# A group of four sorted lanes for one of five: expert weights through SyncE at a row held in a register

## The chip, the cores and the metric

The kernel runs on one core of one Trainium2 chip. The metric is the device time of the run in microseconds (us), and the figure quoted is the median of three runs. Engines are named as the profile names them: PE is TensorE's matrix multiply and PEld its weight load, DVE is VectorE, ACT is ScalarE, POOL is GpSimd, and SP is SyncE, which does nothing here but issue transfers.

## The reference

A decoder of two layers works on x of 16 sequences x 128 tokens x 256 features in float32, with residual additions. Everything but the last step is the same before and after the change; the last step is the one that the change is about.

```python
x = x + attention(layernorm(x), qk, ov)             # layer 0: one head, causal
x = x + cross_attention(layernorm(x), ctx, mask)    # 16 heads of 16
x = x + block_ffn(layernorm(x))                     # router over 16 blocks of 64, the best 4 kept
x = x + (self_attention(layernorm(x)) + b_o + layernorm(x))   # layer 1: 16 heads
x = x + windowed_attention(layernorm(x), cell)      # windows of 64, rotary, causal and same cell
x = x + moe(layernorm(x))

def moe(x):                                         # x: (2048, 256)
    scores = sigmoid(x @ gate.T)                    # 8 experts
    w, idx = top_k(scores, 2);  w = 2.5 * w / w.sum(-1)
    g, u = einsum('th,eih->tei', x, w_gate), einsum('th,eih->tei', x, w_up)    # i: 128
    y = einsum('tei,ehi->teh', silu(g) * u, w_down)
    routed = einsum('te,teh->th', one_hot_weights(w, idx), y)
    return routed + swiglu(x, ws_gate, ws_up, ws_down)          # shared expert of width 256
```

Each token needs two of the eight experts.

## The kernel before

**Lanes and threads.** The 16 sequences are eight lanes of two (`NL`, `G`), so that a lane is 256 tokens. Each lane goes through layer 0 and layer 1. In Python every lane's layer is a generator, called a thread here, which yields the name of the engine that it wants next and the buffers that it needs for that step. The class `Turns` holds these threads while the kernel is built. It keeps a model of when each engine comes free (`free_at`), when each thread can go on (`th.at`), and when each buffer of a kind comes free. `Turns.run` takes, over and over, the thread with the lowest key, lets it issue its step, and charges the modelled cost: `SWITCH` for a change of the matmul's shape, `HOP` for a passage from one engine to another, `RELEASE` for a buffer's return. So the order of every engine's queue is written out when the kernel is built, and on the chip each engine works through its queue in that order, waiting where an operand is late.

Before the change, `key` lets a thread that holds or asks for an attention score buffer (`first`) go ahead by `LEAD` = 100 ns. `LIMITS` gives how many buffers there are of each kind: five `xn` (normalised tokens), three `qs` (masked queries), six `p`. The buffers `p` of 128 x 1024 float32 serve three users: the attention's exponentials, a tile of the experts (as `we`), and a lane's gathered results (as `yg`).

**Which lanes run at once.** `more` begins lane-layers in the order `TURN`: layer 0 of lanes 0 to 5, then by turns layer 1 of a lane and layer 0 of a later one. Up to `IN_FLIGHT` = 6 lane-layers run at once. A masked query or a rotated key needs a swap of neighbouring rows, which is a transfer that SP issues (`q.load`, line 189, buffer `swap`). So SP's queue holds the swaps, the loads of mask rows, and the stores of results.

**The experts.** There are two ways. A lane that is in no group goes dense: `expert_ffn` multiplies all of its 256 tokens by all eight experts and both halves of the shared one (`gu`), weights each expert's hidden values by `wb`, and adds the ten products of `y`. A lane in `GROUPS` goes sorted. `routing` ranks its experts, multiplies 0/1 selections into counts (`n`) and scatters each token's row twice into `to_experts` in memory, with four indirect transfers that POOL issues (`q.indexed`, line 168). The shared expert is a thread of its own (`shared`). When the last lane of the group has been routed, `sorted_experts` starts. Its `plan` is a row of small DVE steps that finds, for each tile of 128 rows, the expert and the first row; it leaves `tile_rows` and `tile_weights`, one index for each partition. Then all tiles start at once as threads of `expert_tile`. Five lanes make 27 tiles: 5 x 256 x 2 rows are 20 tiles, and 7 more are needed because every expert's rows begin a new tile.

A tile takes one `p` buffer. POOL first gathers the expert's weights into three quarters of it, by `tile_weights`, and then the tokens into the last quarter, by `tile_rows`. PE transposes the tokens (`xgt`), multiplies gate and up (`gu2`), transposes the hidden values (`hT2`) and multiplies down (`y2`). ACT copies the result over the tokens and stores it to `by_experts` on its own queue. When all tiles are stored, `combining` gathers four times per lane from `by_experts` (`yg`, by POOL), and DVE adds each, weighted, to `x`; SP stores the lane's output (line 1194, and line 1336 for a dense lane).

**Lines.** Most operations go through helpers of `Turns`, so the profile shows the helper's line: L135 a matmul, L140 a transpose, L144 DVE, L149 ACT, L155 POOL, L168 an indirect transfer, L189 a load or store.

Of the kernel before, what the change touches and what calls it, by code (L numbers as in the profile page):

```python
# [17 lines left out]
B, S, D = 16, 128, 256  # L18
P = 128
# [11 lines left out]
BPC = P // 64  # L31
NE, TOPE = 8, 2

GROUPS = ((0, 1, 2, 3, 4),)


OUT = -(2.0**100)
# [37 lines left out]
PE, DVE, ACT, POOL, SP = "PE", "DVE", "ACT", "POOL", "SP"  # L75
# [6 lines left out]
class Turns:  # L82
# [3 lines left out]

    LEAD = 100.0
    HOP = 70.0  # L90
    HOP_FROM_PE = 200.0
    SWITCH = 91.0
    PART = 20.0
    RELEASE = 30.0

    def __init__(self, nc, limits):
        self.nc = nc
# [22 lines left out]
    def shaped(self, shape):  # L120

        if shape != self.shape:
            self.shape = shape
            self.charge(PE, self.SWITCH)

# [31 lines left out]
    def moved(self, n_bytes):  # L157

        self.moves = max(self.moves, self.now.at) + n_bytes / 300.0
        self.now.at = self.moves + 2000.0  # L160

    def indexed(self, out, out_index, src, src_index):

        at = lambda i: None if i is None else bass.IndirectOffsetOnAxis(ap=i, axis=0)
        self.charge(POOL, 1050.0)
        self.moved(4 * int(np.prod((src if src_index is None else out).shape)))
        self.now.at += 2000.0
        self.nc.gpsimd.indirect_dma_start(out, at(out_index), src, at(src_index))  # L168

    def fetch(self, out, src):  # L170
# [58 lines left out]
    def run(self, more):  # L229

        while True:
            more()
            best = None
            for i, th in enumerate(self.threads):
                if th.ask is None:
                    continue
                engine, takes = th.ask
                at = self.reach(th, engine)
                ok = True
                for tag, n in takes.items():  # L240
                    left = sorted(self.tiles[tag])
                    if not n:
                        continue
                    if len(left) < n:
                        ok = False
                        break
                    at = max(at, left[n - 1])
                first = th.holds or "s" in takes
                tiled = engine == PE and self.shape != WHOLE and ("s" in takes or "oT" in takes)
                key = (max(at - self.LEAD * first, self.free_at[engine] - first), not first, not tiled, th.rank, i)  # L250
                if ok and (best is None or key < best[0]):
                    best = key, th, at
            if best is None:
                assert not self.threads, "no thread can go on"
                return
            _, th, at = best
            engine, takes = th.ask
            for tag, n in takes.items():
                self.tiles[tag].sort()
                del self.tiles[tag][:n]  # L260
            th.at, th.last = max(th.at, at), engine
            if engine == PE:
                self.free_at[PE] += self.PART
            self.resume(th, None)
# [10 lines left out]
def decoder(ctx: ExitStack, tc: tile.TileContext, a: dict, out: bass.AP):  # L275
# [19 lines left out]
    rows = keep.tile([P, N_ROWS], F32, name="rows")  # L295
# [11 lines left out]
    first = wts.tile([P, 4, DC, D], F32, tag="f3", name="first")  # L307
# [30 lines left out]
    experts = keep.tile([P, NE, P], BF16, name="experts")  # L338
# [20 lines left out]
    class Sorted:  # L359
# [16 lines left out]

    groups = [Sorted(k, lanes) for k, lanes in enumerate(GROUPS)]
    group_of = {l: g for g in groups for l in g.lanes}
# [4 lines left out]


    LIMITS = dict(
        bank=4, s=2, oT=1, xn=5, xT=4, qk=5, qs=3, kb=3, v=3, p=6, oS=2, on=4, xe=3, hm=5, tmp=3,
        rank=2, selT=2, p0=2, pT0=2, unseen=4, chosen=3, swap=1, words=1, top=3,
    )
    q = Turns(nc, LIMITS)
# [685 lines left out]
    def plan(g):  # L1075


        yield DVE, dict(tmp=3)
        T, E1 = g.tiles, NE - 1
        n_full = g.cap // P  # L1080
        little = lambda name, n: small.tile([P, n], F32, tag=name, name=name, bufs=1)
        n = little("n_of", NE)
        q.dve("tensor_tensor", n, g.next_row, g.first_row, ALU.subtract)
        q.dve("tensor_scalar", n, n, 1.0 / P, None, ALU.mult)
        t = new("tmp", [P, NE, n_full], "n_full")
        full = consts[:, C_IOTA : C_IOTA + n_full].unsqueeze(1).to_broadcast([P, NE, n_full])
        q.dve("tensor_tensor", t, along(n, n_full), full, ALU.is_gt)
        tiles = little("tiles", NE)
        q.dve("tensor_reduce", tiles, t, AX.X, ALU.add)
        tri = consts[:, C_TRI8 : C_TRI8 + NE * NE].rearrange("p (e f) -> p e f", f=NE)  # L1090
        t = small.tile([P, NE, NE], F32, tag="n_tri", name="n_tri", bufs=1)
        q.dve("tensor_tensor", t, tri, tiles.unsqueeze(1).to_broadcast([P, NE, NE]), ALU.mult)
        first = little("first", NE)
        q.dve("tensor_reduce", first, t, AX.X, ALU.add)
        q.dve("scalar_tensor_tensor", g.offset, first, float(P), g.first_row, ALU.mult, ALU.subtract)
        end = little("end", NE)
        q.dve("tensor_tensor", end, first, tiles, ALU.add)
        iota = consts[:, C_IOTA : C_IOTA + T]
        each = lambda v: v[:, 0:E1].unsqueeze(1).to_broadcast([P, T, E1])
        past = new("tmp", [P, T, E1], "past")  # L1100
        q.dve("tensor_tensor", past, along(iota, E1), each(end), ALU.is_ge)
        e = little("e_of", T)
        q.dve("tensor_reduce", e, past, AX.X, ALU.add)
        t = new("tmp", [P, T, E1], "t_of")
        q.dve("tensor_tensor", t, past, each(tiles), ALU.mult)
        f = little("f_of", T)
        q.dve("tensor_reduce", f, t, AX.X, ALU.add)
        q.dve("tensor_tensor", f, iota, f, ALU.subtract)
        q.dve("tensor_scalar", f, f, float(P), float(g.cap - P), ALU.mult, ALU.min)
        q.dve("scalar_tensor_tensor", f, e, float(g.cap), f, ALU.mult, ALU.add)  # L1110
        for to, v in ((g.tile_rows, f), (g.tile_weights, e)):
            if v is e:
                q.dve("tensor_scalar", v, v, float(P), None, ALU.mult)
            q.dve("tensor_scalar", v, v, consts[:, C_ROW : C_ROW + 1], None, ALU.add)
            q.dve("tensor_copy", to, v)
        q.give("tmp", 3)

    def expert_tile(g, i):

        yield POOL, dict(p=1)  # L1120

        we = new("p", [P, HC, S], "we").rearrange("p h s -> p (h s)")
        xg = yo = we[:, 3 * D :]
        q.indexed(we[:, 0 : 3 * D], None, a["L1_experts"], g.tile_weights[:, i : i + 1])
        yield POOL
        q.indexed(xg, None, g.to_experts, g.tile_rows[:, i : i + 1])
        yield PE, dict(bank=1)
        t = bank([P, DC, S], "xgt")
        for d in range(DC):
            q.transpose(t[:, d, :], xg[:, d * P : (d + 1) * P], ident)  # L1130
        yield ACT, dict(xe=1)
        xgT = new("xe", [P, DC, S], "xgT")
        q.act("copy", xgT, t)
        q.give("bank")
        yield PE, dict(bank=1, tmp=1)
        gu = bank([P, 2, P], "gu2")
        for d in range(DC):
            wt = we[:, d * D : (d + 1) * D].rearrange("p (n f) -> p n f", f=P)
            q.matmul(gu, xgT[:, d, :], wt, start=d == 0, stop=d == DC - 1)
        q.give("xe")  # L1140
        yield ACT
        sg = new("tmp", [P, P], "sg2")
        q.act("activation", sg, gu[:, 0, :], AF.Tanh, scale=0.5)
        yield DVE, dict(p0=1)
        h = new("p0", [P, P], "h2")
        q.dve("scalar_tensor_tensor", sg, sg, 1.0, gu[:, 0, :], ALU.add, ALU.mult)
        q.dve("scalar_tensor_tensor", h, sg, 0.5, gu[:, 1, :], ALU.mult, ALU.mult)
        q.give("tmp")
        q.give("bank")
        yield PE, dict(bank=1)  # L1150
        t = bank([P, P], "hT2")
        q.transpose(t, h, ident)
        q.give("p0")
        yield ACT, dict(pT0=1)
        hT = new("pT0", [P, P], "hT")
        q.act("copy", hT, t)
        q.give("bank")
        yield PE, dict(bank=1)
        y = bank([P, D], "y2")
        q.matmul(y, hT, we[:, DC * D : 3 * D], start=True, stop=True)  # L1160
        q.give("pT0")
        yield ACT
        q.act("copy", yo, y)
        q.give("bank")
        q.load(g.by_experts[i * P : (i + 1) * P, :], yo, engine=ACT)
        q.give("p")
# [170 lines left out]

    def sorted_experts(g):
        yield from plan(g)
        yield [expert_tile(g, i) for i in range(g.tiles)]  # L1340
        part_ended(g)

# [95 lines left out]
            if g.left == 0:  # L1438
                q.start(sorted_experts(g), 2 * NL + min(g.lanes), at)

    IN_FLIGHT = 6

    TURN = [(0, l) for l in range(6)]
    for l in range(NL):
# [129 lines left out]
```

## Time and profile before

| | us |
|---|---|
| median of three runs | 845.04 |
| lowest and highest run | 844.15, 847.82 |
| the profiled execution's own time | 846.62 |
| its span | 844.8 |
| PE busy in it | 775.1 (92%) |
| DVE busy | 474.6 (56%) |
| POOL busy | 445.4 (53%) |
| ACT busy | 393.0 (47%) |

The profile records one execution. The span goes from its first instruction to its last; what the run's own time has beyond that, 1.8 us, lies around it. The page also counts 7902 matmuls and a mean granted clock of PE of 0.969 of full speed. A busy engine is one with an instruction in work; a row of a group of instructions gives the engine, the operation, what is written from what, the shape and the count.

### The profile page before, as it was taken

How to read it: one execution, taken by the hardware profiler on the slowest of the kernel's cores; microseconds unless marked ns; L12 is line 12 of the kernel's file. 1: busy time of each engine (PE TensorE's matmuls, PEld its weight loads, DVE VectorE, ACT ScalarE, POOL GpSimd, SP SyncE). 2: the span in 40 equal slices, each digit the busy share in tenths (PEclk: the TensorE clock that was granted, in tenths of full speed). 3: DMA queues.
4: the chain of work that ended last, by engine and by line, in shares of the span. 5: the costliest groups of instructions: out<-in, count | busy, mean ns of one | idle time of the engine just before them, and what ended most of it. 6: DMA issues, size and time to landing. Idle time of an engine off the chain costs nothing.

```text
span 844.8 us, 19702 instructions
## 1 busy us (share of the span) xinstructions
PE 775.1 (92%) x7902; PEld 610.1 (72%) x7902; DVE 474.6 (56%) x1201; ACT 393.0 (47%) x874; POOL 445.4 (53%) x688
## 2 busy tenths in 40 slices
PE   6999999999999999999999899989894899988848
PEld 5877777887787876777687677757673577866726
DVE  5455746536654375827817768685667435245533
ACT  4545652533635565555465666547442344233100
POOL 5345654433533474728954678676646735450530
PEclk9999999999999999999999999989897899999969
DMA  9356642231110120001014111110205334551330
GB/s 306 99 158 191 192 118 69 80 103 26 28 38 24 34 77 2 28 26 51 13 65 151 46 45 45 45 38 33 64 33 150 113 101 137 156 181 48 103 94 25
DMA packets 60938, 70.43 MB, mean 83 GB/s; under 512 B 8848, under 2 KB 52496, under 8 KB 60208
## 3 DMA queue, kind: packets, MB, share of 16 engines
q1 hardware_dynamic: 51584, 46.24, 17.7%
q0 software_dynamic: 5376, 19.40, 7.7%
q10 hardware_dynamic: 3888, 3.54, 1.2%
q8 instruction: 62, 1.02, 0.5%
q14 instruction: 28, 0.23, 0.1%
HBM read 43.99 MB, written 20.97 MB: 77 GB/s over the span
## 4 chain that ended last, share of the span: by engine, by line
PE 72%; DVE 10%; POOL 7%; issue 4%; ACT 3%; DMA 2%; another core or an unknown queue 1%; SPq 0%; ACTq 0%; POOLq 0%; DVEq 0%
PE s L135 14%; PE pj L135 11%; PE y L135 9%; PE gu L135 9%; PE pr L135 8%; PE hp L135 7%; PE oT L135 4%; PE tps L140 3%; PE o L140 2%; DVE top L144 2%; POOL rstd L155 2%; POOL we L168 1%; ACT p L149 1%; POOL kb L155 1%
## 5 line engine op out<-in xcount | busy, mean ns | idle before, releaser
L144 DVE TENSOR_REDUCE top<-s 128x8 f32<-128x1024 f32 x96 | 112.8, 1217 | 49.6 <-PE s L135 49.0
L149 ACT ACTIVATE p<-s 128x1024 f32<-128x1024 f32 x96 | 93.2, 1022 | 48.6 <-PE s L135 45.4
L155 POOL TENSOR_TENSOR qs<-qT,less 128x512 f32<-128x512 f32 x48 | 61.4, 1281 | 58.0 <-ACT less L149 57.1
L155 POOL TENSOR_SCALAR rstd<-mv 128x2 f32<-128x2 f32 x77 | 18.6, 242 | 105.2 <-DVE mv L144 97.5
L149 ACT ACTIVATE sg<-gu 128x256 f32<-128x256 f32 (+1 forms) x67 | 22.2, 340 | 98.5 <-PE gu L135 56.3
L135 PE MATMUL hp<-srcT,L_w 128*128 128x256 f32 x256 | 65.2, 384 | 0.0
L135 PE MATMUL s<-kb,qT 32*128 32x256 f32 x768 | 61.2, 407 | 4.0 <-DVE top L144 2.6
L135 PE MATMUL s<-qs,kb 32*128 32x128 f32 x1536 | 58.8, 283 | 4.2 <-DVE top L144 1.4
L135 PEld LDWEIGHTS s<-qs,kb 32*128 32x128 f32 x1536 | 48.9, 186 | 18.1 <-issue 9.3
L155 POOL TENSOR_TENSOR rstd<-rstd,power 128x2 f32<-128x2 f32 x77 | 55.8, 724 | 6.4
L155 POOL TENSOR_SCALAR kb<-kT,consts 128x256 f32<-128x256 f32 x96 | 54.8, 582 | 4.6 <-ACT kT L149 3.6
L135 PE MATMUL y<-L_w,hm 128*128 128x256 f32 x256 | 57.0, 381 | 0.0
L135 PE MATMUL gu<-srcT,gu 128*128 128x256 f32 x192 | 50.4, 414 | 6.2 <-issue 2.6
L135 PE MATMUL oT<-p,v 128*32 128x128 f32 x1536 | 53.3, 278 | 1.3 <-ACT oS L149 0.7
L144 DVE TENSOR_TENSOR x<-x,y 128x512 f32<-128x512 f32 x16 | 11.0, 684 | 76.7 <-PE y L135 76.7
L135 PEld LDWEIGHTS s<-kb,qT 32*128 32x128 f32 x768 | 38.0, 186 | 21.5 <-issue 7.9
L135 PEld LDWEIGHTS y<-L_w,hm 128*128 128x128 f32 x256 | 48.2, 190 | 7.0 <-issue 0.5
L135 PEld LDWEIGHTS hp<-srcT,L_w 128*128 128x128 f32 x256 | 44.5, 191 | 9.8 <-issue 1.7
L135 PEld LDWEIGHTS gu<-srcT,gu 128*128 128x128 f32 x192 | 38.2, 207 | 16.4 <-issue 3.1
L144 DVE SCALAR_TENSOR_TENSOR sg<-sg,gu 128x256 f32<-128x256 f32 (+1 forms) x67 | 24.4, 364 | 44.9 <-ACT sg L149 41.6
L168 POOL DMA_INDIRECT we<-in_L_experts,tile_weights x27 | 26.4, 978 | 43.5 <-ACT hT L149 7.6
L135 PEld LDWEIGHTS oT<-p,v 128*32 128x32 f32 x1536 | 40.0, 111 | 12.9 <-issue 8.9
(216 smaller groups left out, 1791.3 us busy)
## 6 DMA issues: line engine op xcount, KB each, us to landing
to_experts<-zero SPq DMA_DIRECT2D x7, 1280.0 KB
unseen<-hidden SPq DMA_DIRECT2D x128, 64.0 KB
c<-in_ctx SPq DMA_DIRECT2D x16, 256.0 KB
by_experts<-we ACTq DMA_DIRECT2D x27, 128.0 KB
x<-in_x SPq DMA_DIRECT2D x8, 256.0 KB
L_w<-in_L_w SPq DMA_DIRECT2D x2, 1024.0 KB
hidden<-plain SPq DMA_DIRECT2D x32, 64.0 KB
swap<-kT SPq DMA_DIRECT2D x16, 128.0 KB
```

The costliest lines, as they stand in the source:

```text
L135: self.nc.tensor.matmul(out, lhsT, rhs, **kw)
L140: self.nc.tensor.transpose(out, src, ident)
L144: getattr(self.nc.vector, name)(out, *args, **kw)
L149: getattr(self.nc.scalar, name)(out, *args, **kw)
L155: getattr(self.nc.gpsimd, name)(out, *args, **kw)
L168: self.nc.gpsimd.indirect_dma_start(out, at(out_index), src, at(src_index))
```

## The change

Seven things change.

1. Lane 4 leaves the group and goes dense. The sorted group has four lanes, and 23 tiles.
2. A tile's order is turned round: POOL gathers the tokens first. The weights then come by one plain transfer that SP issues. Its source row depends on the expert, so SP first reads that row's number from `tile_weights` into a register (`value`), and the transfer's address is computed from it.
3. In the built order a step that needs gathered rows comes later: `indexed` charges 3500 ns after the transfer for 2000, and `sorted_experts` adds 3000 ns after the plan.
4. `IN_FLIGHT` is 5 for 6.
5. There are six `xn` buffers for five, and two `qs` for three.
6. The key has no `LEAD` and no comparison with the engine's free time; it is the time at which the step can start, then the same order of preferences as before.
7. `SWITCH` is 115 for 91, `RELEASE` 0 for 30. These, like the charges under 3, are numbers of the builder's model and put no instruction into the kernel.

```diff
-GROUPS = ((0, 1, 2, 3, 4),)
+GROUPS = ((0, 1, 2, 3),)
...
-    LEAD = 100.0
...
-    SWITCH = 91.0
+    SWITCH = 115.0
...
-    RELEASE = 30.0
+    RELEASE = 0.0
...
+    def value(self, src, most):
+
+        self.charge(SP, 400.0)
+        return self.nc.values_load(
+            src, engines=(mybir.EngineType.SP,), min_val=0, max_val=most,
+            skip_runtime_bounds_check_because="a count of the experts but one, times their rows",
+        )
+
     def indexed(self, out, out_index, src, src_index):
...
-        self.now.at += 2000.0
+        self.now.at += 3500.0
...
-                first = th.holds or "s" in takes
                 tiled = engine == PE and self.shape != WHOLE and ("s" in takes or "oT" in takes)
-                key = (max(at - self.LEAD * first, self.free_at[engine] - first), not first, not tiled, th.rank, i)
+                key = (at, not (th.holds or "s" in takes), not tiled, th.rank, i)
...
-        bank=4, s=2, oT=1, xn=5, xT=4, qk=5, qs=3, kb=3, v=3, p=6, oS=2, on=4, xe=3, hm=5, tmp=3,
+        bank=4, s=2, oT=1, xn=6, xT=4, qk=5, qs=2, kb=3, v=3, p=6, oS=2, on=4, xe=3, hm=5, tmp=3,
...
-        q.indexed(we[:, 0 : 3 * D], None, a["L1_experts"], g.tile_weights[:, i : i + 1])
-        yield POOL
         q.indexed(xg, None, g.to_experts, g.tile_rows[:, i : i + 1])
+        landed = q.now.at
+        yield SP
+        first = q.value(g.tile_weights[0:1, i : i + 1], (NE - 1) * P)
+        q.load(we[:, 0 : 3 * D], a["L1_experts"][bass.ds(first, P), :])
+        q.now.at = max(q.now.at, landed)
...
         yield from plan(g)
+        q.now.at += 3000.0
         yield [expert_tile(g, i) for i in range(g.tiles)]
...
-    IN_FLIGHT = 6
+    IN_FLIGHT = 5
```

## The prediction

> **What bounds the kernel now.** I read the page first, for the engine that is busy and the chain's shares.
>
> ```profile
> span 844.8 us, 19702 instructions
> ...
> PE 775.1 (92%) x7902; PEld 610.1 (72%) x7902; DVE 474.6 (56%) x1201; ACT 393.0 (47%) x874; POOL 445.4 (53%) x688
> ...
> PE 72%; DVE 10%; POOL 7%; issue 4%; ACT 3%; DMA 2%; another core or an unknown queue 1%; SPq 0%; ACTq 0%; POOLq 0%; DVEq 0%
> ```
>
> TensorE (PE) is busy for 775.1 of 844.8 us and carries 72% of the chain. What is to be won is in the 69.7 us in which it stands still, and in the slow clock that follows such gaps. The busy time by stage shows where they are. Its columns are stretch, length, then busy time and count of PE, PEld, DVE, ACT and POOL, granted clock, DMA share and GB/s.
>
> ```profile
> core 0: us, PE busy (x) PEld busy (x) DVE busy (x) ACT busy (x) POOL busy (x), PEclk, DMA share, GB/s
> 0.00:25.00 25.00, 17.80 (x90) 15.29 (x91) 14.42 (x53) 10.65 (x21) 11.58 (x37) 1.00 0.89 301
> 25.00:325.00 300.00, 297.69 (x3230) 238.37 (x3228) 160.22 (x360) 150.06 (x326) 144.69 (x237) 1.00 0.28 84
> 325.00:600.00 275.00, 259.88 (x3302) 199.77 (x3297) 178.63 (x431) 156.37 (x316) 179.54 (x275) 0.98 0.16 50
> 600.00:675.00 75.00, 56.17 (x478) 41.14 (x477) 47.10 (x128) 27.28 (x65) 47.52 (x70) 0.84 0.29 85
> 675.00:800.00 125.00, 116.06 (x703) 93.60 (x701) 56.46 (x190) 45.04 (x136) 53.05 (x64) 0.99 0.39 119
> 800.00:845.00 45.00, 27.52 (x111) 21.92 (x111) 17.73 (x44) 3.62 (x10) 9.05 (x10) 0.84 0.21 66
> ```
>
> PE is idle 7.2 us at the start, 2.3 in the next 300, 15.1 up to 600, then 18.8 in the 75 us from 600 to 675, 8.9 up to 800, and 17.5 at the end. The two worst stages also have the clock at 0.84. The timeline says what the first of them waits for: it is where the sorted group's tiles are about to begin.
>
> ```profile
> 639.73 1.09 PE L140 MATMUL o<-consts,oS 128*128 128x128 f32 x4 [2.90 <-DVE on L144]
> 646.49 1.37 PE L140 MATMUL ot<-consts,xn 128*128 128x128 f32 x4 [5.46 <-DVE xn L144]
> 648.05 0.95 POOL L168 DMA_INDIRECT we<-to_experts,tile_rows  x1 [0.30 <-DMA swap<-kT]
> 653.10 0.52 PE L140 MATMUL xgt<-consts,we 128*128 128x128 f32 x2 [2.32 <-DMA we<-to_experts,tile_rows]
> ```
>
> Lane 4's routing, the plan and the first gathers follow one another, and few lanes are left to fill PE meanwhile. The group's counts are multiplied at 603.9 us, the first tile is transposed at 653.1. The first token gather starts on POOL at 648.05, 5 us before its transpose, behind four gathers of weights. At the end there is one long gap:
>
> ```profile
> 815.11 0.42 DVE L144 TENSOR_TENSOR hm<-wb,hm 128x256 f32<-128x256 f32 x1 [11.65 <-remote]
> 815.59 0.37 PE L135 MATMUL wb<-selT,experts 128*128 128x256 bf16 x1 [10.47 <-DVE hm L144]
> ```
>
> It lies in the burst of twenty gathers of results (786.9 to 811.8 us); who releases it, the profile does not say.
>
> **The change, part by part.** In the built order of the changed kernel 23 tiles are left of 27, SP has 23 register loads and 23 weight transfers, and POOL has no weight gathers.
>
> *Lane 4 goes dense: TensorE work added.* The chain's pieces give the pitch:
>
> ```profile
> 828.43 1.73 PE gu L135 x8
> 830.16 0.11 PE wb L135
> 832.11 8.65 PE y L135 x40
> ```
>
> A 128x256 float32 instruction takes 1.73/8 = 0.216 us. The dense lane adds 64 of gu and 32 of y against its experts, so 96 x 0.216 = 20.7, 8 of wb at 0.11 = 0.9 and 2 more short ones: 21.8 us. A tile has 4 of gu and 2 of y (1.30) and three transposes (0.33), so 1.63 us. Four tiles fewer take away 6.5. Lane 4 also loses its second transposition (4 x 0.11) and five count products (under 0.1 each). The sum is +14.5 us on the bounding engine. Nothing hides it except gaps that it fills.
>
> *The weights leave POOL.*
>
> ```profile
> L168 POOL DMA_INDIRECT we<-in_L_experts,tile_weights x27 | 26.4, 978 | 43.5 <-ACT hT L149 7.6 <-issue 7.6 <-ACT sg L149 7.3
> L168 POOL DMA_INDIRECT we<-to_experts,tile_rows x27 | 25.8, 957 | 7.5 <-issue 6.6 <-PE wb L135 0.3 <-DMA swap<-kT 0.3
> ```
>
> POOL loses 27 x (0.98 + 0.3 between issues) = 34 us of issuing, four token gathers, four scatters and four gathers of results (15 us). The Trainium skill, page "DMA: Bandwidth & Descriptors", section "Issuing engines are not separate DMA queues", speaks against a gain: all transfers run on the same 16 engines, and issuing from several engines only saves the sequencer's issue time, usually small beside the transfer. By the rule this part is worth 0. By the chain's rows between 596 and 705 us, POOL's issue of these tiles is 8.3%, or 9 us. I take the row, in part: four weight issues (5 us) stood before the first token gather and are counted in the gap below; of the other 4 I take 2, as POOL's 43.5 us of waiting for a `we` buffer passes to the token gather, which writes the same buffer.
>
> *What SP takes over.* Each tile's register load stands before its transfer, and six of these pairs stand before the swaps of a late lane's query and key. The trace has no register load. From below it is an SP issue (swap, 1.11 us for two, 0.55); the same page's "Latency and other measured facts" gives a floor of about 0.6 us. Nothing measured gives the upper end; I allow 2 us, about one issue and the 1.5 us that a swap waits at most for an earlier one. With the row six pairs take 6 x (0.55 + 0.4) = 6 us, with 2 us 14. If the first is right, SP is early enough, since it is idle over most of this stage, and PE has 34 us of work between the first tile and the late lane's scores. Queued behind SP's wait are swaps and mask rows of the last lanes: their POOL and DVE rotation waits, then PE. Value taken: +2, ends 0 and +15. A gain through a faster transfer is excluded by the token gather, which must land anyway.
>
> *The gap at 600 to 675.* Counting matmuls at the same pitches, 28 us of PE work stand between the last counts and the first tile in the old order, 39 in the new. In the old trace they took 49 us, so 21 were lost, of which 18.8 shows as idle. The longer cover closes 11, the four weight issues gone from POOL close 5: -16. PE then doesn't fall to half clock at 650 to 660, where about 4 us of speed went: -20 in all. Ends -5 (the lanes' own waits remain) and -24.
>
> *The burst at the end.* Sixteen gathers for twenty: the stall shrinks with it, 17.5 x 4/20, so -3. Here is a new wait too: the last lane's rank operations stand on POOL behind these gathers. From the last tile's product: 0.7 of copy and issue, 3.6 landing (chain), 20 of issue (16 x 1.25), 1 for eq and gt, 3 of small DVE steps, which makes 28 to 29 us, against 28 us of PE work before PE needs the result. +1, ends 0 and +10; if the stall of the old burst repeats, the two overlap.
>
> *Five lanes in flight for six, six xn, two qs, no lead, other constants.* They reorder everything and add no instruction. In the range 325 to 600 there are 15.1 us of idle with six. One chain fewer could raise that by a third (+5) or more; a sixth xn and four scatters fewer take away waits of lanes on scatters (2.65 and 3.72 us on the chain at 375 and 394). I take +1, with ends -8 and +12. The start is untouched.
>
> Sum: +14.5 - 2 + 2 - 20 - 3 + 1 + 1 = -6.5, against 844.8 of span, or 846.62 for that execution. Its median fellow runs at 845.04, and the difference is applied there: 838.5.
>
> **The rivals.**
> 1. *The TensorE work shows in full (slower).* If five lanes in flight leave PE as thin in the late stage as before, the gap only moves to another group of waits: -6 for the gap, -3 for the burst, +14.5 for the work and +4 for reordering give 854. For it: PE at 92% busy, and the gap's causes at 640 and 646 are DVE waits of lanes, not of tiles. Against it: tiles become available 17 us of PE work earlier, with more lanes still running. It decides when less than 14 us of the old gaps is filled.
> 2. *SP becomes the head of line (slower).* A weight transfer waits for its buffer on SP, and the next lane's swap stands behind it. POOL's longest such waits were 5 to 8 us. Two lanes late by 8 us each, on top of the forecast: 838.5 + 16, near 854, up to 862 with 2 us register loads. Against: SP is idle between its few issues.
> 3. *A draw.* Half of the gap is closed (-10) and the rest stands: +14.5 - 10 - 3 - 2 + 4 gives +3.5 or, with the POOL saving in full, 0: 845 to 848.
> That the change doesn't happen is excluded by the built order.
>
> **How the numbers follow.** Forecast with its relatives below 841: 0.46. Draw, within 0.5% of 845.0 (about what a measurement can tell from no change): 0.15. Rival 1: 0.24, rival 2: 0.15. The likeliest case is 838.5, its own range 824 to 841. The range for all reaches to 862, leaving out the ends in which both rivals meet and those in which every gap closes.
>
> **What would show it.** Right: PE's count stays near 7900 with busy time up by 10 to 15 us; idle in the stage of the first tiles falls from 18.8 to under 8 and its clock rises to over 0.95; POOL loses 27 entries of weight gathers. Wrong: SP's register loads last over 1.5 us and swaps are late after them; or PE idle in the middle stage grows past 25 us; or a gap over 15 us stands in the burst of gathers.

## The result and the profile after

The changed kernel takes 856.6 us (median of four runs, 854.18 to 861.14) for 845.3 of the kernel before on the same chip: a ratio of 1.0136, 95% interval 1.0087 to 1.0184. It is slower, where 838.5 us was forecast; the time lies within the stated range and on the wrong side. The runs of this study fell on chips of two kinds, on which the kernel before takes 845 to 849 us or 827 to 829 us, so every ratio below is to the kernel before on the same chip.

The page of the changed kernel has the same lines as before:

```profile
span 855.6 us, 19912 instructions
...
PE 791.6 (93%) x7963; PEld 621.0 (73%) x7963; DVE 481.5 (56%) x1201; ACT 392.3 (46%) x865; POOL 406.2 (47%) x645
...
PE 74%; DVE 15%; ACT 5%; issue 3%; POOL 1%; another core or an unknown queue 1%; DMA 1%; ACTq 0%; DVEq 0%; POOLq 0%
```

PE is 16.5 us busier. POOL lost its 39 us and left the chain (7% to 1%); DVE's share of the chain rose from 10 to 15%, and PE's from 72 to 74%. Taking POOL off the chain did not shorten it. The busy time by stage, in the columns used before:

```profile
0.00:25.00 25.00, 17.58 (x86) 15.01 (x87) 13.73 (x50) 10.74 (x21) 10.96 (x36) 1.00 0.85 300
25.00:325.00 300.00, 293.40 (x3176) 232.51 (x3174) 157.31 (x350) 145.59 (x315) 137.85 (x225) 1.00 0.26 75
325.00:600.00 275.00, 257.04 (x3046) 196.76 (x3046) 178.06 (x417) 148.82 (x306) 171.85 (x265) 0.99 0.14 47
600.00:675.00 75.00, 62.20 (x670) 46.52 (x668) 44.81 (x118) 36.97 (x85) 38.92 (x58) 0.91 0.27 88
675.00:800.00 125.00, 117.94 (x797) 94.37 (x795) 62.06 (x195) 44.02 (x127) 39.06 (x53) 1.00 0.32 101
800.00:856.00 56.00, 43.46 (x197) 35.84 (x197) 25.55 (x72) 6.11 (x17) 7.59 (x9) 0.91 0.15 48
```

The stage of the first tiles did improve: idle 12.8 us for 18.8, clock 0.91 for 0.84. But the two stages before it, where no tile runs, became worse: idle 6.6 for 2.3 us and 18.0 for 15.1, and by 600 us PE has started 6308 matmuls (86, 3176 and 3046) for 6622.

Idle time alone misses the slow stretches, so I use one more measure, **time lost**: the time less the TensorE work started up to it. The work is the matmuls of the trace, each at the pitch of its shape (0.216 us for 128x256 float32, 0.108 for bfloat16, 1.08 for sixteen `s<-kb,qT`, and so on). It adds up to 719.0 us before and 733.5 after, the +14.5 of the prediction.

| | work | lost by 600 us | 600 to 675 | 675 to 800 | 800 to the end | span |
|---|---|---|---|---|---|---|
| before | 719.0 | 55.0 | 31.3 | 17.7 | 21.8 | 844.8 |
| changed | 733.5 | 68.2 | 24.2 | 13.7 | 16.0 | 855.6 |
| difference | +14.5 | +13.2 | -7.1 | -4.0 | -5.8 | +10.8 |

A second pair of traces, from another chip (e5 and e6 below), gives +11.7, -9.7, -2.8 and -7.1, so the split holds within 3 us.

The first tiles in the trace of the changed kernel:

```profile
624.76 0.18 DVE L143 CAST tile_weights<-e_of 128x23 int32<-128x23 f32 x1
625.74 4.94 SPq L196 DMA_DIRECT2D we<-in_L_experts  x6
628.53 1.10 POOL L175 DMA_INDIRECT we<-to_experts,tile_rows  x1 [0.49 <-issue]
635.80 0.59 ACT L148 COPY srcT<-tps 128x512 f32<-128x512 f32 x1 [6.99 <-remote]
636.44 3.89 PE L134 MATMUL gu<-srcT,L_shared 128*128 128x256 f32 x11 [2.48 <-ACT srcT L148]
643.39 0.38 PE L139 MATMUL xgt<-consts,we 128*128 128x128 f32 x2
```

The weights start 0.8 us after the plan. The first tokens are gathered from 628.53, and PE reaches the tile at 643.39 without a wait for them: among PE's waits of this stage no gather is left, where before they made 2.7 us. Still 24 us are lost here, 12.8 of them idle, mostly in waits of lanes such as that of `gu` for `srcT`, which stood behind a releaser that the profile doesn't know. The stretch that the prediction set out to close runs from the group's last counts to the first tile. Its start, before and then in the changed kernel:

```profile
603.89 0.22 PE L135 MATMUL n<-sel,ones 128*128 128x8 bf16 x3
```

```profile
578.60 0.22 PE L134 MATMUL n<-sel,ones 128*128 128x8 bf16 x3
```

So it took 49 us before (603.9 to 653.1) and takes 65 now (578.7 to 643.4). The longer cover is there, 39 us of work as forecast for 28, but the stretch now loses 26 us for 21. The end is the other half of the story (start, length, engine, tile, line and count of each piece of the chain):

```profile
813.52 11.20 PE y L134 x40
...
824.83 3.51 PE gu L134 x16
...
843.04 8.65 PE y L134 x40
```

From 813.5 us on, PE runs dense experts without a gap for 38 us. In this stretch there is nothing left to fill: a lane more of this work here is a lane more of time.

### The profile page after: what moved, and what is told of

It reads as the page before. It is cut to its first block, busy times and chain, and to the rows that moved or that the text cites. A ratio compares the mean times of both kernels' runs of the same rounds, so it can differ in the third digit from the quotient of the medians.

```text
span 855.6 us, 19912 instructions
## 1 busy us (share of the span) xinstructions
PE 791.6 (93%) x7963; PEld 621.0 (73%) x7963; DVE 481.5 (56%) x1201; ACT 392.3 (46%) x865; POOL 406.2 (47%) x645
## 4 chain that ended last, share of the span: by engine, by line
PE 74%; DVE 15%; ACT 5%; issue 3%; POOL 1%; another core or an unknown queue 1%; DMA 1%; ACTq 0%; DVEq 0%; POOLq 0%
PE s L134 14%; PE y L134 13%; PE gu L134 11%; PE pj L134 10%; PE pr L134 8%; PE hp L134 6%; DVE top L143 5%; PE oT L134 4%; PE tps L139 2%; PE o L139 2%; ACT p L148 2%; DVE xn L143 1%; DVE st L143 1%; POOL rstd L154 1%; PE o L134 1%
## 5 line engine op out<-in xcount | busy, mean ns | idle before, releaser
L134 PE MATMUL s<-kb,qT 32*128 32x256 f32 x768 | 64.2, 407 | 5.0 <-ACT p L148 3.6
L134 PE MATMUL gu<-srcT,gu 128*128 128x256 f32 x256 | 60.3, 384 | 1.4 <-DVE hm L143 0.4
L148 ACT ACTIVATE sg<-gu 128x256 f32<-128x256 f32 (+1 forms) x71 | 24.5, 351 | 80.9 <-PE gu L134 66.3
L154 POOL TENSOR_SCALAR kb<-kT,consts 128x256 f32<-128x256 f32 x96 | 53.0, 563 | 3.2 <-ACT kT L148 2.4
L134 PEld LDWEIGHTS gu<-srcT,gu 128*128 128x128 f32 x256 | 46.8, 190 | 10.4 <-ACT we L148 1.0
L143 DVE SCALAR_TENSOR_TENSOR sg<-sg,gu 128x256 f32<-128x256 f32 (+1 forms) x71 | 26.5, 373 | 42.7 <-ACT sg L148 36.0
L175 POOL DMA_INDIRECT we<-to_experts,tile_rows x23 | 22.8, 992 | 53.2 <-ACT srcT L148 12.0
```

The lines of the kernel that those rows point to most:

```text
L134: self.nc.tensor.matmul(out, lhsT, rhs, **kw)
L143: getattr(self.nc.vector, name)(out, *args, **kw)
L148: getattr(self.nc.scalar, name)(out, *args, **kw)
L154: getattr(self.nc.gpsimd, name)(out, *args, **kw)
```

## The experiments

Two theories were stated. A: fewer lanes in flight leave TensorE without work (the 13 us lost before 600). B: the dense work of lane 4 shows in full (the first rival of the prediction). A third, C, is that SP's queue holds up late lanes.

**One part at a time, from the old side.** The first run has only the buffers:

```diff
- xn=5, ... qs=3
+ xn=6, ... qs=2
```

> The kernel before with six xn and two qs buffers for five and three, nothing else. It is the step that five lanes in flight need beside them. Theory A (fewer lanes in flight leave TensorE without work) and theory B (lane 4's dense TensorE work of 14.5 us shows in full) both expect no change here: 845 us, within 4. If the run is over 850, two masked-query buffers are a part of the loss.

It took 823.3 us for 827.1, ratio 0.9949 (0.9927 to 0.997). The buffers are no loss; with them TensorE's queue is that of before for its first 70%. The second adds five in flight, all else still old:

```diff
-    IN_FLIGHT = 6
+    IN_FLIGHT = 5
```

> The kernel before with IN_FLIGHT 5 and the six xn and two qs buffers of the first run. The group keeps five lanes, POOL gathers the weights, the key and the builder's numbers are old. Theory A: in the traces, time minus TensorE work at 600 us was 55 before and 68 after, so 13 us are lost to the smaller number of lanes: 857 us (852 to 862). Theory B: 845 (841 to 849), since no TensorE work is added.

It took 873.1 us, ratio 1.0534 (1.0503 to 1.0566), far above both theories. At 600 us 75.3 us are lost, for 49.6 in the first run, and after it 77.2 for 52.5, so that half of the loss lies where theory A saw none. The third run comes from the new side:

```diff
-GROUPS = ((0, 1, 2, 3),)
+GROUPS = ((0, 1, 2, 3, 4),)
```

> The changed kernel with lane 4 put back into the sorted group (27 tiles), all else as changed. Theory B: 14.5 us of TensorE work less, 842 us (838 to 847). Theory A: the group of four pays for itself, its shorter wait for tiles gives back about what its work costs, and the loss lies in the lanes in flight: 852 to 862. A time between, 847 to 852, would say that both hold in part.

It took 839.8 us for 827.1 of before, ratio 1.0142. Its time falls within B's range, but that range was written for a chip on which before takes 845; as a ratio it looks like A. TensorE's queue is the changed kernel's up to 609 us, but the changed kernel did not run on this kind of chip, so this run decides nothing; e9 and e11 below, on one chip, do. The fourth changes only the way of the weights; TensorE's order is that of before:

```diff
-        q.indexed(we[:, 0 : 3 * D], None, a["L1_experts"], g.tile_weights[:, i : i + 1])
+        q.charge(POOL, 1050.0)
+        q.moved(4 * P * 3 * D)
+        q.now.at += 2000.0
+        first = nc.values_load(g.tile_weights[0:1, i : i + 1], ...)
+        nc.sync.dma_start(we[:, 0 : 3 * D], a["L1_experts"][bass.ds(first, P), :])
```

> The kernel before, with only the way of a tile's weights changed: SP reads the row into a register and issues one plain transfer, in the place where POOL gathered; the builder's model still charges POOL as before, so TensorE's order is that of before and what differs is the chip's doing. Theories A and B: 843 us (839 to 847), 2 us gained as in the prediction. Rival C (SP's queue holds up the swaps of late lanes): 850 to 860.

822.0 us, ratio 0.992 (0.9892 to 0.9948). C falls for the order of before: SP's way is a gain of its own there.

**The same on another chip, and the key.** 

> The changed kernel as it is, on the chip of the other runs of this call. On the first chip its trace had two stalls with an unknown releaser, 8.8 and 2.2 us, and the kernel before had 11.7 to 15.2 us of them in its last gathers; the runs of the first study, on another chip where the kernel before takes 827 us, had none. If those stalls hid a part of the loss, the changed kernel is over 1.4% slower than before here: a ratio of 1.02 to 1.03. If the stalls come with the kernel, the ratio stays at 1.014.

> The kernel before as it is, for its trace on this chip and for the scatter between two copies of one kernel: a ratio of 1.000 within 0.3%. If the chip makes the stall of the last gathers, the gap of 10 us at 815 us of the first trace is gone on a chip where the kernel takes 827 us, and it is there on one where it takes 845.

The changed kernel took 855.4 us, ratio 1.0078 (1.005 to 1.0106), lower than either value expected; the copy of before took 849.2, ratio 1.0002. The long waits with unknown releaser are there again in both, up to 20.3 us in before (15.2 on the first chip) and 10.9 in the changed kernel. They stayed away in all traces from the quicker chips. Run e7 puts the new key, SWITCH and RELEASE on five in flight and five sorted lanes, weights by POOL:

> The second run (five lanes sorted, five in flight, six xn and two qs buffers, weights by POOL) with the new key and the new SWITCH and RELEASE. The second run was 5.3% slower than the kernel before, the changed kernel with five lanes sorted only 1.4%. If the new key gives back what five in flight lose, this one is at 1.5 to 2.5% over the kernel before. If the later places of gathers or SP's transfers do it, it stays at 4 to 6%.

858.6 us for 848.8, ratio 1.0099 (1.0059 to 1.0138). The ratio is flattered, because before stalls in its last gathers on this chip and this run doesn't. By the time lost at 600 us, 66.5 for 75.3, this order gives back a third of what five in flight lost against the first run's 49.6; whether the new key does it, or any other redrawn order would, is not shown. And the candidate, e1 and e4 together:

> A candidate: the kernel before (six in flight, five lanes sorted, old key) with the two parts that gained alone, six xn and two qs buffers (0.5%) and a tile's weights by SP in the place of POOL's gather (0.8%). If the two add up, 1.3% faster than before (1.0 to 1.6%). If both only fill the same gap at the first tiles, 0.8%.

822.2 us for 848.8: ratio 0.9692 (0.9664 to 0.9719), more than the sum, as its last gathers stalled for about 6 us where before stalls for 20.

**Lanes in flight and lane 4, in the new order.** With SWITCH 110 for 115 the builder finds an order for five and for six in flight; these four runs share a chip (before 828.6). The first is the control, and each of the others differs from it in one part:

```diff
-    SWITCH = 115.0          # all four, against the changed kernel
+    SWITCH = 110.0
...
-    IN_FLIGHT = 5           # e10
+    IN_FLIGHT = 6
...
-GROUPS = ((0, 1, 2, 3),)   # e11
+GROUPS = ((0, 1, 2, 3, 4),)
...
-        first = q.value(...); q.load(...)          # e12
+        q.charge(SP, 400.0); q.charge(SP, 350.0); q.moved(4 * P * 3 * D)
+        nc.gpsimd.indirect_dma_start(we[:, 0 : 3 * D], ...)
```

> The changed kernel with the builder's SWITCH at 110 for 115. With 115 the builder finds no order for six lanes in flight and a group of four; with 110 it finds one for each of this run and the next two, so that they differ in one part only. Theory A and theory B: about the changed kernel, 0.5 to 2% over the kernel before on the same chip, and a TensorE-free sum (time minus TensorE work) of 66 to 70 us at 600 us.

> The run before this one (SWITCH 110, group of four) with IN_FLIGHT 6 for 5. Theory A (fewer lanes in flight leave TensorE without work): 10 to 20 us faster than with five, and at 600 us the time lost is at 50 to 57 us, for 68. Theory B (the dense TensorE work of lane 4 shows in full): within 5 us of it, because that work is there in both.

> SWITCH 110, five in flight, lane 4 back in the sorted group (27 tiles). Theory B: 14.5 us faster than with the group of four (10 to 18). Theory A in its pure form: within 4 us of it, the shorter stage of the first tiles and of the last gathers paying for the added TensorE work. The first study, on another chip than the second, had 1.4% for this against 0.8% for the group of four, which stalls of the last gathers make unsure.

> SWITCH 110, five in flight, group of four, and the weights gathered by POOL, issued where SP's transfer stood and charged in the builder's model as SP's, so that TensorE's order is the same as in the first run of this call. What differs is the chip's doing. In the order of before SP's way gained 0.8%, that is 6 us with 27 tiles; for 23 tiles 5 us: this run is 3 to 8 us slower than the first. Rival C (SP delays the swaps of late lanes, which POOL's gathers would not): 3 us faster or more.

| | us | ratio to before, interval | lost by 600 us | lost after |
|---|---|---|---|---|
| e9, four sorted, five in flight | 846.2 | 1.0224 (1.0167 to 1.028) | 68.6 | 42.1 |
| e10, six in flight | 864.4 | 1.0459 (1.0417 to 1.0501) | 79.6 | 49.5 |
| e11, five sorted | 830.0 | 1.0017 (1.0 to 1.0035) | 67.8 | 44.0 |
| e12, weights by POOL | 848.6 | 1.0277 (1.023 to 1.0323) | 64.4 | 47.7 |

Theory A falls: with six lanes in flight the new order is 18 us slower, not 10 to 20 faster. PE's waits between 25 and 600 us (total, times, longest) show a part of the reason; first five in flight (e9), then six (e10):

```profile
PE tps L139 <- DVE xn L143: 4.2, 1, 4.2
...
PE s L134 <- DVE top L143: 2.6, 5, 1.1
```

```profile
PE s L134 <- DVE top L143: 6.5, 4, 3.8
PE ptt L134 <- DVE chosen L143: 5.4, 2, 4.2
PE tps L139 <- DVE xn L143: 3.2, 2, 1.9
```

These are a few long waits for single DVE steps. Some are the order's doing: the step waited for 3.8 us stood behind a row of small steps of other lanes in DVE's queue. The longest is not. The step itself lasted 5.69 us, where its median is 0.21:

```profile
466.45 5.69 DVE L143 TENSOR_SCALAR chosen<-rank 128x32 bf16<-128x32 f32 x1
472.20 0.39 PE L134 MATMUL ptt<-ident,chosen 128*128 128x128 bf16 x2 [4.22 <-DVE chosen L143]
```

Waits for such stretched steps (the last section has more on them) add up to 7.4 us by 600 in e10 and to none in e9. Even without them e10 would lose about 72 us by 600 (79.6 - 7.4, an estimate), where theory A expected 50 to 57. Theory B holds here: TensorE's queue is the same in e9 and e11 up to 594 us, lane 4 dense costs 16.2 us (846.2 for 830.0), and its work is 14.5. In e12 it is that of e9 throughout, so the 64.4 for 68.6 lost by 600, before any tile, is the scatter of this measure, about 4 us; the run points the way of e4 (2.5 us), with intervals that overlap.

**Does the order alone do this, and does lane 4 cost as much in the old one?** The first of two runs is e1 with one number of the builder's model changed, which puts no instruction in or out; the second makes lane 4 dense on top.

```diff
-    RELEASE = 30.0           # both, against e1
+    RELEASE = 20.0
...
-GROUPS = ((0, 1, 2, 3, 4),) # e14
+GROUPS = ((0, 1, 2, 3),)
```

> The kernel before with six xn and two qs buffers and RELEASE 20 for 30 (the builder finds an order with it for five sorted lanes and for four): old key, six in flight, five lanes sorted, weights by POOL. It is the control of the next run: 0 to 1% faster than the kernel before, as the first run, and 48 to 56 us lost at 600 us. If it is over 1% slower, a small change of the builder's numbers alone moves the time by as much as the changed kernel's order did.

> The run before this one with lane 4 dense, in the old order with six in flight. Theory B (the dense TensorE work shows in full): 14 to 18 us slower than it, as in the new order (846.2 for 830.0). The forecast on record (a closed gap of 20 us at the first tiles pays for it): 3 to 10 us faster. At 600 us the time lost should be the control's within 5 us under both.

e13 took 843.2 us for 827.9: ratio 1.0183 (1.0143 to 1.0224), where e1 had 0.9949. A number of 10 ns in a model costs 2.3% (1.0183 for 0.9949). By stage, e1 first and then e13:

```profile
325.00:600.00 275.00, 262.24 (x3366) 202.45 (x3360) 181.78 (x446) 157.05 (x320) 184.59 (x283) 0.99 0.15 49
```

```profile
325.00:600.00 275.00, 255.95 (x3150) 194.38 (x3149) 181.66 (x421) 149.79 (x305) 173.98 (x270) 0.98 0.14 46
```

The two queues of TensorE part at their middle. PE then starts 216 matmuls fewer between 325 and 600 us, with the same work in all; 61.7 us are lost by 600 for 49.6, and 62.9 after it for 52.5.

e14 took 848.1 us, ratio 1.0258 (1.0209 to 1.0307): 4.8 us over its control, between the two forecasts, and in the profiled executions the two spans are equal (843.4 and 843.6). The mechanism of the prediction is there: the time lost after 600 falls from 62.9 to 35.7 us, which pays for the 14.5 of work. But the new order also loses 74.2 us by 600 for 61.7, and the gain is gone. The expectation that the time lost by 600 would stay within 5 us was wrong: making a late lane dense redraws the order hundreds of us ahead of it (26.5 us are lost by 300 us, for 18.9).

**The last gathers.** In e17 the gathers of results are spaced:

```diff
+            for _ in range(2):
+                nc.gpsimd.memset(y[:, i, :], 0.0)
             q.indexed(y[:, i, :], None, g.by_experts, by[:, i : i + 1])
```

> The kernel before with two memsets on POOL ahead of each of the 20 gathers of results, on the quarter of the buffer that the gather then fills (0.31 us each by the trace of before), so that the gathers are 1.9 us apart for 1.25; all else stands in the same order. If back-to-back gathers hold up TensorE's reports of completion, then on a chip where the kernel before takes 845 to 849 us the gaps with unknown releaser (8 to 20 us) fall under 4 us and the time by 5 to 15 us, though the burst itself is 12 us longer. If something else stalls, the gaps stay. On a chip where the kernel before takes 827 us there is no stall to remove: 0 to 12 us slower, by what of the longer burst is not covered.

This chip was of the slower kind (before 845.5), and e17 took 851.3, ratio 1.0077 (1.006 to 1.0094). The waits with unknown releaser are gone, but the gain of 5 to 15 us did not come, nor is the time lost gone: 15.9 us between 800 and 825, for 17.3 in before. In its place stands a wait that can be read:

```profile
801.94 0.48 DVE L144 SCALAR_TENSOR_TENSOR x<-yg,weight,x 128x256 f32<-128x256 f32 x1 [1.44 <-DMA yg<-by_experts,results]
802.34 0.68 DVE L144 TENSOR_TENSOR x<-x,y 128x512 f32<-128x512 f32 x1
803.08 3.78 PE L135 MATMUL gu<-srcT,gu 128*128 128x256 f32 x8 [4.64 <-DVE x L144]
```

DVE adds each gathered result in the order of its queue; the dense lane's `x<-x,y` stands behind such an add, and PE waits for it. The gathers' pace becomes PE's. Why, on one kind of chip, back-to-back gathers make ACT and DVE wait for something unknown stays open.

**The candidate again.**

> The candidate again (six xn and two qs buffers, weights by SP, all else as before). On the chip where the kernel before takes 849 us it was 3.1% faster, because there the last gathers stalled less. If this chip is of the other kind (before at 827), 0.8 to 1.4% faster; if of the first kind, about 3% again.

814.6 us for 827.9, ratio 0.9852 (0.9812 to 0.9892): faster than the kernel before on both kinds of chip, with six in flight, five sorted lanes and the old key. The changed kernel ran on the slower kind alone; there the candidate took 822.2 us (e8) and it took 855.4.

## Why the prediction was wrong, step by step

In the traces the change cost 10.8 us of span where -6.5 was forecast, so the sum was off by 17.3. Two terms failed, about equally: the reordering by 12.2 us and the gap at the first tiles by 12.9. The stages after 675 us came out 7.8 better than their terms.

- **TensorE work, +14.5.** Right: 733.5 for 719.0, and PE 16.5 us busier. That gaps pay for it was the error. In the new order the time lost after 600 us is 44.0 with lane 4 sorted (e11) and 42.1 with it dense (e9): there was no gap left to fill, and 16.2 us show.
- **The reordering, +1 (ends -8 and +12).** This step failed, beyond its own ends. In the changed kernel 13.2 us more are lost by 600, before a tile exists. 7.1 of them are idle time (6.6 and 18.0 for 2.3 and 15.1); the rest is PE at a lower pace, at a granted clock no lower than before (1.00 and 0.99), and what slows it stays open. "One chain fewer", the working's reason for a loss, is not enough to explain it: with five in flight the old order loses more (75.3 for 49.6), but in the new order it is six that lose more (79.6, of which 7.4 are waits for stretched steps, for 68.6). The traces whose order up to 500 us is that of before (before, e1, e4, e6, e8, e15, e17) lose 49.6 to 56.3 us by 600; every order built here that parts from it earlier, e13's with its single number among them, loses 61.7 to 79.6. A redrawn order was costed at a near-zero mean; measured, all eleven runs with one (seven different orders up to 594 us, as some share theirs) lost 7 to 25 us more by 600 than before did. Whether the order of before was picked among many is not shown by any run, but it would explain why each redraw lost.
- **The gap at 600 to 675, -20 (ends -5 and -24).** This step failed too, within its ends. It gave -7.1, with 12.8 us idle (under 8 was forecast) and a clock of 0.91 (over 0.95). The tile's own part was right: the first tile no longer waits. The error is in "the longer cover closes 11": the cover came, but it is lanes' work with waits of its own, and the stretch from the last counts to the first tile loses 26 us for 21. So the outcome is near the end of -5, for which the prediction had named "the lanes' own waits remain". (A reading to set right: the half clock stands mostly at 640 to 650 us, where 0.50 was granted; 650 to 660 has 0.83.) The next stage gave 4.0 more that the sum did not have.
- **The burst, -3, and +1 for the rank operations behind it.** 5.8 us came back at the end, and a shorter stall fits that: in before, three waits of 11.7 to 15.2 us with unknown releaser, after, one of 8.8. The rank operations cost nothing, as PE runs without a gap from 813.5 us on. On the quicker chips there was no stall to shorten. The changed kernel was not run there; e9, which differs from it in SWITCH and so in its order from 193 us on, has 1.0224.
- **SP's register loads, +2 (0 to 15), and POOL's issue, -2.** A register load takes 0.27 us by the trace below; the prediction assumed 0.55, beside the floor of about 0.6 that it cites from the Trainium skill, and here the measurement decides. Six transfers with the loads between them take 4.94 us (6 assumed). The net was not zero but a gain of 0.8% in the order of before (e4), of about 1% with the buffers (0.9852 for 0.9949), and 2.5 us, not clear of noise, in the new. Against the Trainium skill's "DMA: Bandwidth & Descriptors", section "Issuing engines are not separate DMA queues", which makes moving the issue to another engine worth little, the prediction took its row and gave POOL's part 2 us: one plain transfer for an indirect one, and 27 gathers off POOL, were worth 5 to 9 us here (e4 against before, e15 against e1). Which of the two did it was not separated, so the page's sentence, which speaks of the issue alone, is not refuted.

```profile
L164 SPq TENSOR_LOAD <-tile_weights x23: 263/273/485, 625.0 to 743.4; - x23
```

The numbers are minimum, median and maximum in ns. None of the signs listed as "wrong" came up: register loads are short, the middle stage idles 18.0 and not over 25 us, and no gap over 15 us stands in the gathers. A loss spread over 600 us in waits of 1 us and slower pace has no single sign. The first rival named the right end (854, for a median of 856.6), in part by luck: it had +4 for the reordering, where 13.2 was measured, and 6.8 too little for what the stages after 675 us gave back. (The draw's sum, too, does not reach 0: +3.5 less the other 2 us of POOL's issue is +1.5.)

## What to carry to other kernels

Where a builder writes the queues, a change of its numbers or of what it schedules can redraw all of them, and the new order is to be costed against the order that it replaces: here 7 to 25 us more were lost by 600 us, and a change of 10 ns in the model alone cost 2.3%. Test a part with the order held (as in e4 and e12), or beside a control whose order is redrawn without the part (as in e13), before a gain or a loss is put down to the part. Work put in front of a late operand covers the wait only if that work does not wait itself. And work added on the bounding engine is paid for only by a gap that is still there after the rest of the change has been made.

## What the hardware showed

A small DVE step can take many times its length while POOL works without a pause. In the trace of e2:

```profile
374.07 6.31 DVE L143 TENSOR_SCALAR chosen<-rank 128x32 bf16<-128x32 f32 x1
374.76 2.48 POOL L154 TENSOR_TENSOR x<-x,rows 128x512 f32<-128x512 f32 x2
377.19 0.71 POOL L154 TENSOR_TENSOR x<-x,on 128x256 f32<-128x256 f32 x1
377.87 1.25 POOL L154 TENSOR_TENSOR qs<-qT,less 128x512 f32<-128x512 f32 x1
379.09 1.25 POOL L154 TENSOR_TENSOR xn<-xn,rows 128x512 f32<-128x512 f32 x1
380.44 0.39 PE L134 MATMUL ptt<-ident,chosen 128*128 128x128 bf16 x2 [6.15 <-DVE chosen L143]
```

The step's median in that trace is 0.18 us. It ends with the fifth POOL instruction in a row, and PE waited 6.15 us for it. In e10 the same step lasted 5.69 us and ended with the fourth in a row (its lines are above). The Trainium skill's "SBUF — State Buffer", section "SBUF: two separate sides", tells of a port that DVE and POOL share under an exclusive lock, held for one instruction; here DVE seems to have stood through four and five. In the changed kernel one such step (`xn`, 3.52 us for 0.41) made PE wait 1.46 us at 605 us. No run took POOL's work away to test it, so the lock is the likely cause and not a shown one.

The other surprise is the chip: one kernel, with the same instructions, takes 827 us on one and 849 on another, and the same edit gains 3.1% on the slower kind (e8) and 1.5% on the quicker (e15).
